# Rows of Z with 514 words instead of 528 in a two-layer graph network

## The chip, the cores and the metric

The kernel runs as one program on one core of a Trainium2 chip. The metric is device time in microseconds: the time before is the median of three executions. A fourth execution was recorded by the hardware profiler; the lines called "profile" are from it.

## The reference

There are 3125 nodes with 256 features and 50,000 directed edges (src, dst) with 16 features each; the edges are sorted by dst. Two graph layers are applied, each on the normalised, rectified nodes and each added back:

```python
# layer 0: message passing, summed at the source node
h = relu(layernorm(x))
msg = relu(concat(h[src], h[dst], edge_attr) @ mW1 + mb1) @ mW2 + mb2
agg = segment_sum(msg, src)
x = x + h + relu(concat(h, agg) @ uW1 + ub1) @ uW2 + ub2
# layer 1: three graph convolutions with self loops
h = relu(layernorm(x))
for W, b in ((W1, b1), (W2, b2), (W3, b3)):
    h = D^-1/2 (A + I)^T D^-1/2 (h @ W) + b    # gelu after the first two
x = x + h
```

## The kernel before

`mW1` has three parts, so the first product of a message is a sum of three terms: one that depends on the source node alone (table `tabA`), one on the target node alone (table `tabB`, with the bias in it) and one on the edge's features. The kernel calls **Z** the sum of the last two, 512 words for each edge. The edges come sorted by target; the sums at the source nodes need them sorted by source. So Z is written out in the order of the targets, each row to a place that belongs to its source tile, and is read back in that order.

**The array of rows.** `rows_d` (L112) lies in HBM. It has 25 tiles of source nodes (125 nodes each) of CAP = 17 x 128 rows, and spare rows behind them for edges that have no place. A row has ZW words of 4 bytes (L68): H = 512 words of Z, two words of `ends` (the source's number within its tile, plus one, and the target's number, plus one), and, before, 14 words that are zero. Nothing reads those 14.

**Stage one: blocks.** `for b in range(NB)` (L775) goes over 66 blocks of 768 edges, six columns of 128 edges each. `window` (L617) has SP load the block's two windows of `tabB` into `bw`; `features` has ACT load edge features; `prepare` (L632) makes the one-hot matrices. `block` (L656) works the six columns one after the other: GpSimd copies the block's `ends` into `zt` (L659), TensorE multiplies the one-hot matrix with the window (L666), ScalarE or VectorE copies the product into `zt` (L669), and GpSimd issues an indirect DMA that scatters the 128 rows to their places in `rows_d` (L670). `zt` is a ring of RZ = 4 buffers, each of 128 partitions x 6 rows of ZW words; the four buffers were filled with zero beyond word 514 by one GpSimd memset each (L599). They lie in memory that the tiles of the kernel's lead-in (`l1`) used, and which is given back at L591.

Rows 14 x 128 to 17 x 128 of a tile may stay without an edge. They are filled with zero by 25 DMAs of SP from the tile `zero` (L285), 384 rows each, six ahead of the blocks and the others in every second block. Scatters of the blocks from 48 on wait for all the fills.

From block 26 on (FULL_AT) the first five groups of 128 rows of every source tile are complete, and from block 29 on `first_sums` (L712) works on them beside the blocks. `rows_of` (L699) has SP load a tile's 640 rows into `xz` (L702), a ring of two buffers, one tile ahead. VectorE makes the one-hot matrices from the two words behind Z (L744 to L748), TensorE turns them and expands `tabA` (L252), VectorE adds Z (L254), ScalarE and VectorE split the rectified message in two parts (L256, L257), and TensorE sums over the edges of each source (L734). The one-hot matrices are kept for later as `oh_d`, rows of 630 half-precision words (L760). Work on the node tables (L325 to L370) is spread over the blocks ahead of block 26.

**Stage two: messages.** `messages` (L880) does the same for the other twelve groups of 128 rows of each tile, four groups in one load: `load_rows` (L891) has SP load 512 rows into `z` (L894), a ring of three buffers, two loads ahead. Beside them it counts the adjacency matrix (L950) and updates the nodes.

**Stage three.** `gcn` (L1217) is the three graph convolutions, with the adjacency matrix as the multiplied operand. It does not use the rows of Z.

The order of instructions on an engine is that of the program; the tile framework adds the waits on semaphores. DMAs of one issuing engine share a queue: q0 in the profile is GpSimd's, q1 SP's, q10 ScalarE's.

Of the kernel before, what the change touches and what calls it, by code (L numbers as in the profile page):

```python
# [45 lines left out]
N, D, H, ED, E = 3125, 256, 512, 16, 50000  # L46
# [18 lines left out]
MID = 1024  # L65
NG, AW = 7, 448
NPAD = NG * AW
ZW = 528  # L68
ROWS = NT * CAP
EPS = 1e-5  # L70
assert NT * NP == N and EP * EC == E and N <= NPAD
# [31 lines left out]
def gnn(ctx: ExitStack, tc: tile.TileContext, x, src, dst, ea, mW1, mb1, mW2, mb2, uW1, ub1, uW2,  # L103
        ub2, W1, b1, W2, b2, W3, b3, out):
    nc = tc.nc
# [5 lines left out]

    rows_d = dram.tile([ROWS + P * MB * NB, ZW], F32, name="rows_d")  # L112
    tabA = dram.tile([NR * P, H], F32, name="tabA")
# [28 lines left out]
    HALF = 13  # L142
    XZ = max(HALF * D, KP * ZW)
    xh = [g1.tile([P, XZ], F32, name="xz", bufs=2)[:, :HALF * D].rearrange("p (c f) -> p c f", f=D)
# [119 lines left out]
    with s1:  # L264
# [14 lines left out]

        zero = g1.tile([P, ZW], F32, name="zero")  # L280
        nc.gpsimd.memset(zero, 0.0)
        fills = []

        def fill(t, after=None):
            f = nc.sync.dma_start(  # L285
                rows_d[t * CAP + SURE:(t + 1) * CAP, :].rearrange("(i p) w -> p i w", p=P),
                zero.unsqueeze(1).to_broadcast([P, KT - SURE // P, ZW]))
            if after is not None:
# [274 lines left out]
        i = 2 * NT  # L563
# [32 lines left out]
        zt = []  # L596
        for i in range(RZ):
            zt.append(z1.tile([P, MB, ZW], F32, name=f"zt{i}"))
            nc.gpsimd.memset(zt[i][:, :, H + 2:], 0.0)  # L599
        EB = 6  # L600
        st, one, pay, made, evicted = {}, {}, {}, {}, {}

# [96 lines left out]
        def rows_of(t):  # L699
            v = g1.tile([P, XZ], F32, name="xz", bufs=2)[:, :KP * ZW]  # L700
            v = v.rearrange("p (k w) -> p k w", w=ZW)
            o = nc.sync.dma_start(  # L702
                v, rows_d[t * CAP:t * CAP + KP * P, :].rearrange("(k p) w -> p k w", p=P))
            tc.declare_no_dep(o.ins, group="late rows", reason="the other blocks have none of these")
            tc.add_to_no_dep_group("first loads", o.ins)
            for c in ready:
                tc.add_manual_dep(o.ins, c.ins.name, SYNC, reason="all rows are in place")
            a = a_rows[t % 2]
            nc.sync.dma_start(a, tabA[t * NP:(t + 1) * NP, :])
            return v, a  # L710
# [697 lines left out]
```

## Time and profile before

| | |
|---|---|
| median of 3 runs | 2078.67 us (2077.79 to 2092.57) |
| profiled execution | 2082.0 us |
| its span, first to last instruction | 2080.3 us |
| mean granted TensorE clock | 0.933 |
| busy, share of the span | PE 89%, PEld 67%, DVE 61%, ACT 52%, POOL 21% |
| DMA | 359.09 MB in 189,439 packets |
| q0 (GpSimd: the scatters, nearly all) | 108.12 MB, 13.5% of 16 engines' span |
| q1 (SP) | 211.58 MB, 32.0% |
| first scatter, last scatter | 71.0 us, 787.5 us |
| first load of stage two | 798.2 us |

The profile gives microseconds from the first instruction of one execution. Engines are PE (TensorE's matmuls), PEld (its weight loads, which run beside them), DVE (VectorE), ACT (ScalarE), POOL (GpSimd) and SP (which only issues DMAs). The granted clock is the share of TensorE's full clock that the throttle gave. The DMA share is the mean busy share of the core's 16 DMA engines. A line such as "L669 ACT COPY" names the line of the kernel below. A wait is written as engine, what it was about to do, "<-", and what released it; "issue" stands where the profile shows nothing that it waited for. Behind the lines the trace also has a record of every DMA packet, with its queue, its size, its start and its duration.

### The profile page before, as it was taken

To read this page: it belongs to the slowest core of one execution; us is meant where nothing else is said; L and a number is where in the kernel's file an instruction comes from. 1 tells how busy PE (TensorE), PEld (TensorE's weight loads), DVE (VectorE), ACT (ScalarE), POOL (GpSimd) and SP (SyncE) were. 2 spreads that over 40 slices of the span, in tenths; PEclk is the share of its full clock that TensorE was granted. 3 is DMA by queue.
4 is the path that set the end of the run, shared out by engine and by line. 5 is a ranking of instruction groups with operands and counts; after the bars stand their busy time and mean duration, and the time that the engine had idled before them with its cause. 6 is when DMAs were issued, how large, how long until landed. Compare 5 with 4: busy or idle time off the path is not lost. (4 is left out here: it accounts for less than half of the span.)

```text
span 2080.3 us, 28281 instructions
## 1 busy us (share of the span) xinstructions
PE 1856.0 (89%) x9183; PEld 1399.1 (67%) x9183; DVE 1271.6 (61%) x2855; ACT 1071.6 (52%) x2214; POOL 442.3 (21%) x522
## 2 busy tenths in 40 slices
PE   4788686568989996999999999999979999999997
PEld 2433343344545554688888888888867998999996
DVE  7886244455655555998888898889833223323332
ACT  3454355555666563556555565555536344434342
POOL 5466477554555441000000000000000000000000
PEclk9788898788998887999999999999989999999998
DMA  8689799897888876544544545544321000000111
GB/s 263 236 329 372 275 355 351 297 328 255 298 304 289 277 257 223 163 152 154 160 147 141 164 145 160 150 156 142 108 75 49 1 1 1 1 1 8 32 39 49
DMA packets 189439, 359.09 MB, mean 173 GB/s; under 512 B 38224, under 2 KB 67776, under 8 KB 188890
## 3 DMA queue, kind: packets, MB, share of 16 engines
q1 hardware_dynamic: 122790, 211.58, 32.0%
q0 software_dynamic: 31760, 108.12, 13.5%
q10 hardware_dynamic: 34724, 37.42, 5.3%
q8 instruction: 76, 1.25, 0.2%
q14 instruction: 89, 0.73, 0.1%
HBM read 187.51 MB, written 169.47 MB: 172 GB/s over the span
## 5 line engine op out<-in xcount | busy, mean ns | idle before, releaser
L1254 PE MATMUL p_o<-a,g 125*128 125x448 f32 x2100 | 462.8, 375 | 2.2 <-ACT g L1239 2.0
L670 POOL DMA_INDIRECT rows_d<-zt,place x391 | 388.9, 995 | 310.2 <-issue 196.6
L1254 PEld LDWEIGHTS p_o<-a,g 125*128 125x128 f32 x2100 | 391.4, 188 | 44.4 <-DVE g L1240 6.0
L256 ACT ACTIVATE m<-gb 128x512 fp32r<-128x512 f32 x425 | 265.6, 632 | 157.4 <-DVE gb L254 105.6
L257 DVE SCALAR_TENSOR_TENSOR m<-gb,m 128x512 fp32r<-128x512 f32 x425 | 287.2, 687 | 34.1 <-ACT m L256 32.4
L1249 ACT CAST a<-A 125x448 fp32r<-125x448 uint8 x263 | 148.6, 565 | 231.4 <-PE p_o L1254 231.3
L1249 DVE CAST a<-A 125x448 fp32r<-125x448 uint8 x262 | 102.8, 393 | 235.2 <-PE p_o L1254 234.3
L993 PE MATMUL p_sum<-m,oh 128*125 128x512 f32 x600 | 234.9, 434 | 6.2 <-ACT m L256 4.6
L950 PE MATMUL p_A<-od,oh_h 128*126 128x448 f16 (+3 forms) x1000 | 237.1, 327 | 1.1 <-ACT of_src L981 1.1
L252 PE MATMUL p_x<-apc,ohT 125*128 125x512 f32 x600 | 235.6, 466 | 1.3 <-ACT ohT L926 0.7
L669 ACT COPY zt<-p_z 128x512 f32<-128x512 f32 x339 | 186.9, 587 | 80.3 <-PE p_z L666 74.8
L254 DVE TENSOR_TENSOR gb<-z,p_x 128x512 f32<-128x512 f32 x300 | 202.0, 682 | 33.6 <-PE p_x L252 32.2
L666 PE MATMUL p_z<-bw,ohd 128*128 128x512 f32 x391 | 183.5, 516 | 30.6 <-DVE zt L669 12.9
L1202 POOL DMA_DIRECT2D wG<-in_L_gnn_W x3 | 2.2, 744 | 759.2 <-DVE ln_nmr L239 757.7
L734 PE MATMUL p_sum<-m,hT 128*125 128x512 f32 x250 | 110.7, 489 | 56.1 <-DVE m L257 52.6
L666 PEld LDWEIGHTS p_z<-bw,ohd 128*128 128x128 f32 x391 | 78.5, 210 | 121.7 <-issue 60.8
L950 PEld LDWEIGHTS <-oh_h 128*126 128x126 f16 x1000 | 125.6, 137 | 34.7 <-issue 1.0
L993 PEld LDWEIGHTS p_sum<-m,oh 128*125 128x125 f32 x600 | 111.7, 188 | 48.4 <-ACT m L256 21.6
L936 DVE TENSOR_SCALAR od<-iota_h,dloc 128x447 f16<-128x447 f16 (+11 forms) x300 | 138.5, 487 | 0.0
L974 ACT CAST A<-p_A 126x448 uint8<-126x448 f32 x175 | 92.9, 531 | 59.8 <-PE p_A L950 58.1
L252 PEld LDWEIGHTS p_x<-apc,ohT 125*128 125x128 f32 x600 | 109.2, 193 | 13.0 <-DVE gb L254 1.9
L356 PE MATMUL p_z<-wAB,hT 128*128 128x512 f32 (+1 forms) x200 | 111.4, 695 | 7.2 <-ACT hT L339 3.7
(268 smaller groups left out, 2748.5 us busy)
## 6 DMA issues: line engine op xcount, KB each, us to landing
z<-rows_d SPq DMA_DIRECT2D x75, 1056.0 KB
xz<-rows_d SPq DMA_DIRECT2D x25, 1320.0 KB
rows_d<-zero SPq DMA_DIRECT2D x25, 792.0 KB
tabB<-t_sb ACTq DMA_DIRECT2D x26, 512.0 KB
bw<-tabB SPq DMA_DIRECT2D x51, 256.0 KB
bw<-tabB SPq DMA_DIRECT2D x80, 128.0 KB
rows_d<-zt,place POOLq DMA_INDIRECT x391, 6.3
hT<-tabA SPq DMA_DIRECT2D x25, 250.0 KB
```

Source lines behind the costliest of these rows:

```text
L252: nc.tensor.matmul(p, ohT, apc[:NP, s, :], start=s == 0, stop=s == 1)
L254: nc.vector.tensor_add(gb, zr, p)
L256: nc.scalar.activation(m[:, 0, :], gb, AF.Relu)
L257: nc.vector.scalar_tensor_tensor(m[:, 1, :], gb, 0.0, m[:, 0, :].bitcast(F32), op0=ALU.max, op1=ALU.subtract)
L666: nc.tensor.matmul(p, one[b][:, j, :], bw[(2 * b + j // MH) % RW], start=b < WIDE, stop=True)
L669: evicted[b] = by(z[:, j, :H], p)
L670: s = nc.gpsimd.indirect_dma_start(out=rows_d, in_=z[:, j, :], in_offset=None, out_offset=bass.IndirectOffsetOnAxis(ap=place[:, j, b:b + 1 ...
L936: nc.vector.tensor_scalar(targets[k][:, :WIDTH[k]], iota_h[:, :WIDTH[k]], d_of[:, t, k:k + 1] if k < KP else dloc[t][:, k:k + 1], None, op ...
L950: nc.tensor.matmul(p_A[g][:, l - g * AW:h - g * AW], oh_h[t][:, k, :], targets[k][:, l - FIRST[k]:h - FIRST[k]], start=start, stop=stop)
L993: nc.tensor.matmul(p_sum[t], oh, m[:, s, :], start=k == KP and s == 0, stop=k == KT - 1 and s == 1)
L1249: (nc.vector.tensor_copy if turn[0] % 2 else nc.scalar.copy)(a, A[:NP, s, j * AW:(j + 1) * AW])
L1254: nc.tensor.matmul(po[:, f, :AW], g[:, s, q, f * P:(f + 1) * P], a, start=s == 0 and q == 0, stop=s == NT - 1 and q == 1)
```

## The change

A row of Z has 514 words: the 512 of Z and the two of `ends`. The array `rows_d`, the buffers `zt`, `zero`, `z` and the view of `xz` follow from the constant, and the memsets of the empty words are gone.

```diff
-ZW = 528
+ZW = H + 2
...
         for i in range(RZ):
             zt.append(z1.tile([P, MB, ZW], F32, name=f"zt{i}"))
-            nc.gpsimd.memset(zt[i][:, :, H + 2:], 0.0)
```

A row was 2112 bytes and is 2056. The buffer of `xz` keeps its size, which is set by the node features that used it before (13 x 256 words).

## The prediction

> **What bounds the kernel now.** I read the share line by slices first, then the busy time by stretches, then who waits for whom, then the DMA queues, and last the DMA packets one by one. Stage one (71 to 790 us: the blocks of 768 edges, and beside them the sums over the first five groups of rows) is where rows of Z are written; stage two (790 to 1545) only reads them; the GCN layers (1545 to 2080) do not touch them. The stages, in busy time by stretches (columns: stretch, its length, busy us and instructions of PE, weight loads, DVE, ACT, POOL, granted clock, DMA share, GB/s):
>
> ```profile
> 71.00:330.00 259.00, 202.25 (x626) 96.58 (x626) 143.62 (x342) 124.20 (x248) 165.61 (x190) 0.88 0.90 330
> 330.00:790.00 460.00, 376.27 (x1286) 215.64 (x1285) 260.89 (x498) 276.16 (x542) 240.32 (x267) 0.85 0.84 292
> 790.00:1500.00 710.00, 686.85 (x4308) 571.55 (x4309) 623.96 (x1414) 407.15 (x914) 0.00 (x0) 0.98 0.50 155
> ```
>
> In stage two PE works 687 of 710 us and DMA half the time: PE is the bound, cheaper reads of Z cannot show. In stage one no engine is full (PE 78 and 82%) and DMA stands at 0.90 and 0.84, so the transfers come closest to the bound. Finer stretches show where they are it:
>
> ```profile
> 130.00:220.00 90.00, 70.68 (x221) 33.26 (x220) 56.33 (x129) 40.11 (x81) 57.49 (x67) 0.88 1.02 378
> 220.00:250.00 30.00, 20.32 (x53) 9.87 (x52) 8.41 (x15) 10.99 (x22) 12.95 (x15) 0.73 0.55 198
> 250.00:380.00 130.00, 91.12 (x319) 49.05 (x317) 50.00 (x96) 67.12 (x136) 92.17 (x107) 0.89 0.97 349
> 380.00:480.00 100.00, 66.00 (x247) 41.64 (x248) 60.11 (x115) 57.87 (x115) 45.96 (x52) 0.80 0.82 289
> ```
>
> At 130 to 220 and 250 to 380 the 16 engines are full. The waits of 330 to 790 say who feels it:
>
> ```profile
> POOL rows_d L670 <- issue: 130.3, 106, 12.3
> DVE d_of L744 <- DMA xz<-rows_d: 77.9, 19, 14.1
> ...
> POOL rows_d L670 <- ACT zt L669: 64.0, 55, 11.4
> ```
>
> DVE waits 77.9 us in 19 of 25 tiles for a load of Z rows (xz). POOL's "issue" includes a 0.30 us gap before every scatter, even back to back; only the long ones could be a full queue. POOL has a floor of its own: a scatter is 0.96 us and that gap, so six and the copy of L659 take about 7.8 us; many blocks between 250 and 330 us start 7.8 us apart. There POOL, not DMA, may set the pace.
>
> **What the change does, part by part.**
>
> **Bytes.** A row goes from 2112 to 2056 bytes, -2.65%. From the DMA queues and issues:
>
> ```profile
> q1 hardware_dynamic: 122790, 211.58, 32.0%
> q0 software_dynamic: 31760, 108.12, 13.5%
> ...
> z<-rows_d SPq DMA_DIRECT2D x75, 1056.0 KB
> xz<-rows_d SPq DMA_DIRECT2D x25, 1320.0 KB
> rows_d<-zero SPq DMA_DIRECT2D x25, 792.0 KB
> ```
>
> The packet records of the trace give one packet's time. Scatters travel as packets of 4224 bytes (two rows), median 164 ns; a row of SP's transfers is a packet of 2112 bytes, median 86. Packets of 1024 bytes take 46 and of 2048 take 84, so a packet is 8 ns + 0.0371 ns per byte (2112 bytes: 86.4; 4224: 164.8). By that line 2056 bytes take 84.3 ns, and a pair (4112) 160.6. Estimates: -2.1 ns per row read or filled, -4.2 per pair scattered. In 71 to 790 us the trace has 24,987 pairs and 23,296 single rows (xz and fills): (24,987 x 4.15 + 23,296 x 2.1) / 16 engines = 6.5 + 3.1 = **9.5 us** of DMA time. The 38,400 rows that stage two reads save 38,400 x 2.1 / 16 = 5 us, behind PE: nothing. If that cover were gone, 5 us is all there is.
>
> **How much lies on the path.** 130 to 220 and 330 to 380 us are full: their part, 1.2 + 0.9 us, counts whole. 250 to 330 (1.2 us) is full too, but POOL keeps its 7.8 us floor: I count nothing. The remaining 6.2 us lie where the share is about 0.8: half, 3.1, because DVE waits for the load in 19 of 25 tiles. Sum 5.2, rounded **-5 us**.
>
> **Removed memsets.** Four of 168 ns on POOL at 69.7 us. The first scatter waits for ACT (70.1 us) after that, so they are covered by L669: 0. Without cover, 0.5 us once.
>
> ```profile
> 69.67 0.49 POOL L599 MEMSET zt<- 128x84 f32 x4 [21.68 <-PE bc L651]
> 70.11 0.19 POOL L659 COPY zt<-ends 128x12 f32<-128x12 f32 x1
> 71.00 1.23 POOL L670 DMA_INDIRECT rows_d<-zt,place  x1 [0.69 <-ACT zt L669]
> ```
>
> The wait for the memory's former readers (21.68 us) moves to the copy behind it on the same engine, no later. Scatters, loads and fills keep their number and order; DVE, ACT and PE handle the same elements, only at another row pitch.
>
> **Alignment, the part with no row of its own.** 2112 is 33 x 64; rows of Z start at multiples of 64 bytes now, of 8 afterwards, and neighbours share a 64-byte piece. No row of Z shows that. The nearest rows: oh_d, rows of 1260 bytes, starting at multiples of 4: 3,200 packets written, median 55 ns, mean 55.7, 90th percentile 55, while the scatters run beside them; and 3,200 read back, median 55. The line gives 54.8. hT_d, rows of 12,500 bytes, is written in 468 ns (line: 472). So an odd start costs an engine 0 to 1 ns.
>
> Two rules of the Trainium skill bear on it. "DMA: Bandwidth & Descriptors", How a descriptor splits into AXI transactions, says a read starts at the 256-byte boundary below, and bytes ahead of the row cost beats of 32 bytes. By it a row of Z now costs 66 beats + 3 of lead on average = 69, afterwards about 68.5: 0.6 ns gained instead of 2.1 per row read. But by the same rule the odd reads of oh_d would need 43.75 beats instead of 40, some 60 ns by the line's slope; they took 55, at the 10th percentile and the 90th. The row decides: 2.1. The two differ by 1.5 ns x 16,000 rows of xz / 16 = 1.5 us.
>
> The rule that speaks against the change: "Collectives: The Full Stack", Rules for kernel authors, wants buffers aligned to 32 bytes, which "Prevents HW read-modify-write". It states no price. The oh_d row does not show one, but it writes 128 neighbouring rows in a burst, not scattered rows for 700 us. Bounds per written row: below, -1 ns (the fit's spread); above, 18 ns, if each end becomes a small write of its own (the 4-byte packets take 9 ns). I take 0 to 1, the row in hand, and keep 18 for the range.
>
> **Sum.** Profiled execution: 2082.0 us (span 2080.3 and 1.7 around it), 3.3 above the median of the runs, 2078.67. 2082.0 - 5 = 2077.0; against the median, **2074 us**, -0.25%. About 1% (21 us) is what a measurement of this kernel tells from no change, so this counts as within it.
>
> **Rivals.**
>
> - **The writes pay for their ends (slower).** Place: the scatters of L670 and the fills of L285. At 18 ns per row: 24,987 pairs x 36 / 16 = +56 us, 19 fills of 384 rows x 18 / 16 = +8 us. Of the 64, the part in the full stretches (9,546 of the pairs, 38%) and half of the rest lie on the path, about +44; less the 5 gained: **2118 us**, +39. It passes 1% from 21 + 5 = 26 us on the path, that is 26 / 44 x 18 = 11 ns per row. For it: DMA is full where most scatters lie, so there is no slack, and the rule above. Against: the 55 ns of oh_d. Chance 0.38.
> - **The bytes are hidden anyway.** POOL's 7.8 us floor in the early blocks, the chain of sums later: **2079 us**. For it: POOL back to back at 250 to 330; the end of the stage (770 to 810 us) has a DMA share of 0.48. Against: the 77.9 us that DVE waits. Chance 0.12.
> - **More than the bytes comes back.** Single rows take 102.6 ns on average at a median of 86; if the queueing shrinks with the load, all 9.5 us and half of (102.6 - 86) x 23,296 / 16 = 24 us: **2057 us**. For it: full engines. Against: 2.65% less load does not halve a queue. Chance 0.04.
> - **The rows are cut.** 514 has few divisors; were each row sent as two descriptors, a scatter on POOL would take up to 0.96 us more: 391 x 0.96 = +375 us where POOL is the floor, **2450 us**. For it: nothing in the profile; rows of 630 halfwords go as one packet. Chance 0.02. That the change would not take effect at all is shut out: the row length is one constant for all three transfers.
>
> **How the numbers follow.** The forecast (0.44) and the hidden one (0.12) lie within 1%: 0.56. Slower: 0.38 + 0.02 = 0.40. Faster: 0.04. Likeliest 2074, its own range 2066 to 2083. The range must reach into the slower rival, whose price I know only from 0 to 18 ns and whose share on the path could be whole (64 - 5 = +59 us): from 2062 to 2140 about 0.17 is left out.
>
> **What would show it.** Right: packets of 2056 and 4112 bytes with medians of 84 and 160 to 161 ns, some 25,024 pairs of the latter (102.9 MB where they were 105.7), DVE's wait for xz slightly under 77.9 us, blocks still 7.8 us apart at best, stage two unchanged at 687 us of PE. Wrong: a pair of rows at 180 ns or more, a DMA share near 1 beyond 380 us, longer waits of POOL with cause "issue", the end of stage one later than 798 us. If pairs are at 160 and the stage is still longer, the price sits where packet times do not show it (landing of the scatters, now 6.3 us).

## The result, and the profile after

The change makes the kernel slower: 2102.61 us median of 6 runs (2089.92 to 2105.53), against 2078.14 for the kernel before (also 6 runs). The ratio is 1.0117, 95% interval 1.0085 to 1.0149. The profiled execution took 2105.53 us (span 2103.8, granted clock 0.925); before it was 2082.0 (span 2080.3, clock 0.933).

Of the 23.5 us between the two spans, the start of tile 0 of stage two (the first load of `oh_h`: 808.9 us before, 814.7 after) accounts for 5.8, the way from there to the same load of the last tile for 21.8 (675.1 us before, 696.9 after), and the rest of the program gives 4.1 back. So most of the loss is in stage two, where the forecast had nothing at all. From L599 on, lines of the kernel after have a number that is lower by one. The loads of `oh_h` (behind the shape: how many, the shortest, median and longest issue in ns, and the start of the first and the last), and the busy time from the first to the last of them, before and then after (columns as in the prediction):

```profile
L915 SPq DMA_DIRECT2D oh_h<-oh_d x25: 386/456/1787, 808.9 to 1484.0; - x25
808.90:1484.00 675.10, 667.21 (x4187) 555.36 (x4187) 602.67 (x1363) 393.34 (x885) 0.00 (x0) 0.99 0.50 156
...
L914 SPq DMA_DIRECT2D oh_h<-oh_d x25: 348/456/1787, 814.7 to 1511.6; - x25
814.70:1511.60 696.90, 669.62 (x4188) 556.14 (x4186) 603.67 (x1364) 394.75 (x885) 0.00 (x0) 0.99 0.48 148
```

PE does the same work in both (667 and 670 us busy), but it stands idle for 27.3 us where it stood idle for 7.9: 19.4 of the 21.8 us.

Busy time by the stretches of the prediction, of the kernel after:

```profile
71.00:330.00 259.00, 209.46 (x627) 98.52 (x628) 144.27 (x343) 125.33 (x250) 162.70 (x185) 0.86 0.89 320
330.00:790.00 460.00, 379.94 (x1270) 218.86 (x1269) 257.51 (x490) 272.42 (x535) 245.65 (x270) 0.83 0.84 287
790.00:1500.00 710.00, 666.86 (x4149) 551.73 (x4148) 604.96 (x1364) 396.06 (x884) 1.56 (x3) 0.98 0.48 150
```

In the third line PE is busy 667 of the same 710 us where it was 687, at the same clock of 0.98, with 159 fewer matmuls recorded: less of the work fits into the stretch. DMA's share is 0.48 there (0.50 before). In stage one DMA's shares are what they were or a little lower.

The queues, the DMA issues, and the waits of stage one (330 to 790 us), of the kernel after:

```profile
q1 hardware_dynamic: 122790, 207.99, 31.5%
q0 software_dynamic: 31760, 105.31, 13.1%
...
z<-rows_d SPq DMA_DIRECT2D x75, 1028.0 KB
xz<-rows_d SPq DMA_DIRECT2D x25, 1285.0 KB
```

```profile
POOL rows_d L669 <- issue: 118.9, 101, 11.8
POOL rows_d L669 <- ACT zt L668: 70.5, 61, 12.1
DVE d_of L743 <- DMA xz<-rows_d: 65.9, 17, 11.8
```

The bytes went as forecast, with the same number of packets. Packet by packet, a scattered pair (4112 bytes) has a median of 160 ns (164 before) and a single row (2056 bytes) 85 (86 before); there are 25,024 pairs. DVE's wait for `xz` fell from 77.9 us to 65.9, and POOL's waits with the cause "issue" from 130.3 to 118.9.

What is new stands in the waits of stage two (790 to 1500 us). Before:

```profile
DVE oh L917 <- DMA z<-rows_d: 13.9, 15, 1.4
...
PEld p_sum L993 <- DVE m L257: 5.2, 19, 0.5
...
PE p_sum L993 <- DVE m L257: 0.2, 1, 0.2
```

And after:

```profile
DVE oh L916 <- DMA z<-rows_d: 37.1, 24, 3.5
...
PEld p_sum L992 <- DVE m L257: 26.7, 25, 3.4
...
PE p_sum L992 <- DVE m L257: 19.5, 10, 3.0
```

DVE waits 37.1 us for loads of Z, up to 3.5 us at once, where it waited 13.9. TensorE, which bounds this stage, now waits 19.5 us for the message `m` where it waited 0.2: nearly the 21.8 us that the stage grew. The loads are not slower, though: from SP's issue to the end of the last of its 512 packets a load takes 6.25 us on average before and 6.21 after. But DVE gets to the instruction that needs the load sooner, on average 9.3 us behind the issue where it was 9.8. The order in time on DVE shows it. Before (columns: start, length, engine, line, operation, in brackets the idle time and its releaser):

```profile
1166.31 0.69 DVE L257 SCALAR_TENSOR_TENSOR m<-gb,m 128x512 fp32r<-128x512 f32 x1 [0.51 <-ACT m L256]
1166.92 0.68 DVE L254 TENSOR_TENSOR gb<-z,p_x 128x512 f32<-128x512 f32 x1
1168.30 0.68 DVE L917 TENSOR_TENSOR oh<-z,iota 128x500 fp32r<-128x500 f32 x1 [0.70 <-DMA z<-rows_d]
```

The same three instructions of another tile, after, and behind them TensorE in the same stretch:

```profile
1153.91 0.68 DVE L916 TENSOR_TENSOR oh<-z,iota 128x500 fp32r<-128x500 f32 x1 [3.52 <-DMA z<-rows_d]
1154.51 0.68 DVE L257 SCALAR_TENSOR_TENSOR m<-gb,m 128x512 fp32r<-128x512 f32 x1
1155.11 0.68 DVE L254 TENSOR_TENSOR gb<-z,p_x 128x512 f32<-128x512 f32 x1
```

```profile
1155.25 0.79 PE L992 MATMUL p_sum<-m,oh 128*125 128x512 f32 x1 [2.96 <-DVE m L257]
```

Before, DVE works `m`, `gb`, `oh`; after, `oh`, `m`, `gb`. The one-hot matrix `oh` needs a load of Z that has not landed; `m` and `gb` need nothing of that load, but they stand behind `oh` on the same engine and start only after it, and TensorE's sum waits for `m`. The instructions of the two compiled programs, compared engine by engine, confirm that this is the rule and not an accident of one tile: in stage two, DVE has the order m, gb, oh in 24 places and oh, m, gb in one before, and in 13 and 19 after. GpSimd's order is the same in both programs; TensorE's, ScalarE's, DVE's and SP's differ. Nothing in the diff asks for that. The order is not written in the kernel's text: the tile framework chooses it when it builds the program, and for the kernel after it chose another. Whether the shorter rows or the missing memsets moved it was not separated, since no run has one without the other. The sentence of the kernel's description above, that the order of instructions on an engine is that of the program, is wrong.

### The profile page after: what moved, and what is told of

Read it like the earlier page. It is cut to its first block, busy times and chain, and to the rows that moved or that the text cites. A ratio compares the mean times of both kernels' runs of the same rounds, so it can differ in the third digit from the quotient of the medians.

```text
span 2103.8 us, 28241 instructions
## 1 busy us (share of the span) xinstructions
PE 1868.4 (89%) x9183; PEld 1407.6 (67%) x9183; DVE 1270.6 (60%) x2855; ACT 1073.3 (51%) x2214; POOL 447.0 (21%) x518
## 3 DMA queue, kind: packets, MB, share of 16 engines
q1 hardware_dynamic: 122790, 207.99, 31.5%
q0 software_dynamic: 31760, 105.31, 13.1%
## 4 chain that ended last, share of the span: by engine, by line
PE 64%; DMA 20%; DVE 11%; issue 2%; ACT 1%; POOL 1%; SPq 0%; another core or an unknown queue 0%; ACTq 0%; DVEq 0%; POOLq 0%
PE p_o L1253 20%; DMA xz<-rows_d 8%; PE p_x L252 7%; PE p_A L949 6%; DMA z<-rows_d 6%; PE p_sum L992 5%; PE p_z L356 3%; PE p_z L665 3%; PE p_g L1236 3%; PE p_z L664 2%; PE p_sum L733 2%; PE nd L841 2%; PE nd L854 2%; PE nd L863 2%; DVE gb L254 2%
## 5 line engine op out<-in xcount | busy, mean ns | idle before, releaser
L992 PE MATMUL p_sum<-m,oh 128*125 128x512 f32 x600 | 235.5, 436 | 22.5 <-DVE m L257 19.5
```

Of the source, the lines that this page charges most:

```text
L992: nc.tensor.matmul(p_sum[t], oh, m[:, s, :], start=k == KP and s == 0, stop=k == KT - 1 and s == 1)
```

## The experiments

The theories. **O**, the order: the loss comes from the order that the framework gives the changed program, above all from `oh` (also called the mask) ahead of `m` on DVE; the row length by itself costs nothing. **W**, the writes: rows of 2056 bytes pay for ends that do not fill 32-byte pieces (the slower rival of the prediction), in whatever order.

To separate them, a kernel builds both programs, reads off the order of every engine in one, and imposes it on the other by dependencies that exist only while the program is built: they fix who comes first on an engine and add no wait on the chip. Each is compared with the kernel before on the same chip, in five rounds. Three chips were used, and they differ in speed by more than the change does (the kernel before has medians from 2078 to 2111 us), so ratios are compared and not times.

### Short rows, the order of before

```diff
-    nc = bacc.Bacc(...)                        # one program
+    ORDER[:] = order_of(program(528)[0])       # each engine's order with rows of 528 words
+    nc, arrays = program(514)                  # rows of 514 words
...
+    for k, places in ORDER:
+        if k > 0:       # both parts of the program
+            for a, b in zip(places, places[1:]):
+                tc.add_manual_dep(here[MADE[b]], MADE[a], FREE, reason="the other program's order")
```

> Rows of 514 words, with every engine's instructions in exactly the order that the kernel before has. Theory O (the planner that orders the instructions prices a shorter transfer lower, and so laid out another order; that order costs the time, the rows save a little): ratio to before 0.995 to 1.000, 2068 to 2079 us, the first load of stage two at 792 to 798 us, stage two's loads 28.3 us a tile. Theory W (the writes pay for ends that share a 64-byte piece): the time stays with the rows, 1.009 to 1.015, 2097 to 2109 us.

Measured: ratio 0.9992, interval 0.9971 to 1.0013 (2107.03 us against 2108.03 on that chip). From tile 0 to the last, stage two takes 677.9 us. The loss is gone with the rows still short. W's price, if there is one, is no larger than what the bytes bring, to within the interval.

### Long rows, the order of after

The same with the two widths exchanged: rows of 528 words with their memsets, in the order of the kernel after.

> The mirror image: rows of 528 words, with every engine's instructions in the order that the changed kernel has. Theory O: the time stays with the order, ratio 1.010 to 1.016, 2099 to 2111 us, and DVE waits some 35 us in stage two for loads of Z rows. Theory W: 0.998 to 1.003, 2074 to 2084 us.

Measured: 1.0083, interval 1.0052 to 1.0114, a little under the 1.010 to 1.016 expected. Not a byte of the change is in this kernel, and it has the change's waits:

```profile
DVE oh L917 <- DMA z<-rows_d: 36.2, 19, 3.2
...
PEld p_sum L993 <- DVE m L257: 26.3, 22, 3.0
...
PE p_sum L993 <- DVE m L257: 19.8, 10, 2.6
```

The order is enough to make some seven tenths of the loss. That is O, and it shuts out W as its main cause.

### Which part of the order: stage one or the rest

Two kernels take stage one in one order and everything behind it in the other.

```diff
     for k, places in ORDER:
-        if k > 0:       # both parts of the program
+        if k > 1:       # stage two and what follows; stage one stays as the framework orders it
```

First, 514 words with the order of before from stage two on:

> Rows of 514 words; stage one in the changed kernel's order, stage two and the convolutions in the order of the kernel before. If O holds and the loss is made in stage two by its order (there the two profiles part by 21 us, in stage one by 6): stage one ends some 6 us later than before and stage two costs no more than before, ratio 1.000 to 1.004, 2078 to 2087 us. If stage two is slow because of what stage one hands over, or because of the rows: 1.009 to 1.015, 2097 to 2109 us.

Measured: 0.9993, interval 0.9973 to 1.0014. Second, 528 words with the order of after from stage two on:

> Rows of 528 words; stage one in the order of the kernel before, stage two and the convolutions in the changed kernel's order. If the order of stage two carries the loss: ratio 1.007 to 1.012, 2093 to 2103 us, with the first load of stage two at 798 us as before. If it does not (W, or an effect of stage one): 0.998 to 1.002, 2074 to 2082 us.

Measured: 1.0082, interval 1.0058 to 1.0106. The order of stage one shows no effect, within intervals of 0.2% each way; the effect of the order comes from stage two on. An effect of stage one of up to some 6 us (0.3%) would not show here, so the 5.8 us by which stage two starts later in the profile of after have no shown cause. They are within what single profiles differ by: the kernel with the mask put back and the changed kernel run again (both below) have the same orders in stage one and ran on one chip, and their first loads of `oh_h` start at 804.6 and 812.2 us.

### The mask put back

The kernel after, in its own order on every engine, except that on DVE in stage two each `oh, m, gb` becomes `m, gb, oh`:

```diff
-        oh (L916)   m (L257)   gb (L254)
+        m (L257)    gb (L254)  oh (L916)
```

> The changed kernel in its own order, but on VectorE, in stage two, the 19 places where a one-hot (oh) stands right ahead of a message's split (m) and the next message's sum (gb) are turned round to m, gb, oh, as the kernel before mostly has it. Theory H (VectorE waits in order for a load of Z rows at oh, and m and gb stand behind it; TensorE waits for m): ratio to before 0.998 to 1.004, VectorE waits no more than 20 us for loads of Z rows in stage two, stage two 28.3 to 28.6 us a tile. If the order of TensorE or ScalarE carries the loss: 1.007 to 1.014.

Measured: 1.0043, interval 1.0023 to 1.0062; the change itself, run again on that chip (below), 1.0114. Moving this one instruction, in 19 places, gives back 0.7 of the 1.1%; 1.0043 is just above the 0.998 to 1.004 expected if the place of `oh` on DVE were all. The waits of this kernel in stage two say what is left:

```profile
DVE oh L917 <- DMA z<-rows_d: 14.5, 20, 1.4
...
PEld tr L924 <- DVE oh L917: 12.6, 8, 1.6
...
PE tr L924 <- DVE oh L917: 9.4, 9, 1.1
...
PEld p_sum L993 <- DVE m L257: 3.6, 14, 0.5
```

The waits for the load and for `m` are those of before. In their place TensorE waits for `oh`: its own order still has the transposes of `oh` (L924), for 12 of the 75 loads, earlier among its sums than in the kernel before. That fits the remaining 0.4%, but no run changed TensorE's order alone, so it is not shown.

### The mask moved ahead in a kernel that is not slow

The opposite: short rows in the order of before, with each of the 24 `m, gb, oh` turned into `oh, m, gb` on DVE, and nothing else moved.

> Rows of 514 words in the order of the kernel before, with the reverse move: in stage two the 24 places where VectorE has m, gb, oh become oh, m, gb. Theory H: the loss comes back with this move alone, ratio 1.006 to 1.014, VectorE waits 30 us or more for loads of Z rows in stage two. If the place of oh does not matter: 0.996 to 1.002, as with this order unmoved (0.9992).

Measured: 1.0296, interval 1.0263 to 1.0330, the expected direction and twice the expected size; stage two takes 729.5 us from tile 0 to the last. In its waits:

```profile
PEld p_sum L993 <- DVE m L257: 51.8, 33, 3.3
...
DVE oh L917 <- DMA z<-rows_d: 46.6, 22, 3.2
PE p_sum L993 <- DVE m L257: 44.3, 21, 3.1
```

Against the same kernel without the move (0.9992 and 0.9981 on other chips), 3% from one instruction of 0.68 us placed ahead of two others in 24 places. PE's own wait of 44.3 us is most of the 54 us by which the stage is longer than in the kernel before. The rest is that PE is busy for 678.9 us where it was 667.2, at a granted clock of 0.98 where it was 0.99; why was not tested.

### Other row lengths in the order of before

With the order held, the row length can be varied alone. Rows of 544 words (2176 bytes, a multiple of 32):

```diff
-    nc, arrays = program(514)
+    nc, arrays = program(544)
```

> Rows of 544 words (2176 bytes, a multiple of 64 as 2112 is), in the order of the kernel before: 3.0% more bytes a row. If bytes of Z rows lie on the path as the prediction had it (half of the DMA time, -5 us for 56 bytes): +6 us, ratio 1.003. If they are hidden: 0.999 to 1.001. If the full DMA time counts: 11 us, 1.005.

Measured: 1.0073, interval 1.0045 to 1.0102, more than the 1.003 expected. That left open whether short rows gain less than bytes are worth, because of their ends, so three lengths were run together on another chip: 520 words (a multiple of 32 bytes), 546 (not one), and 514 again.

> Rows of 520 words (2080 bytes, a whole number of 32-byte pieces) with every engine held to the order of the kernel before. The step from 528 to 544 words in that order cost 0.73%, 0.046% a word; 514 words in it gave 0.08%. If the price is one of bytes and rows of 2056 bytes pay for ends that are not whole pieces, 520 words show what the bytes alone are worth: 8 x 0.046%, ratio 0.996 (2070 us). If bytes under 2112 are hidden and no ends are paid for, 0.999 to 1.000. In both the tiles of stage two stay at 28.3 us; the difference shows in the time of stage two's first load.

> Rows of 546 words (2184 bytes, not a whole number of 32-byte pieces), order of the kernel before. By bytes alone 18 x 0.046% = 0.8%, ratio 1.008, beside 1.0073 of 544 words (2176 bytes, whole pieces). If the ends of a row are paid for as much as 514 words would have to pay to lose their 0.6%, 1.014. Against 1.008 it would be the alignment that matters, near 1.008 it is not.

> Rows of 514 words in the order of the kernel before, once more, on the chip of the two beside it: 0.9992 as the first time if bytes under 2112 bring nothing; 0.994 if the 0.046% a word that 544 words cost holds below 528 too and the first time was low by chance.

Measured: 520 words 0.9970 (0.9946 to 0.9994), 546 words 1.0042 (1.0020 to 1.0064), 514 words 0.9981 (0.9962 to 1.0000). Alignment does not order them: 546 words cost no more than 544 (on another chip), and 514 and 520 cannot be told apart. The price of 0.046% a word, taken from the 544 words, did not hold: 546 words cost half of the 1.008 that it asked for, and the 0.994 that it asked for with 514 words lies outside the interval.

The load that starts tile 0 of stage two tells how long everything ahead of it took. On the chip of the 544-word kernel it starts at 804.7 us with 514 words (the kernel with the mask ahead) and at 815.5 with 544: 10.7 us for 30 words. On the chip of the other three it starts at 837.1 us with 514 words, 840.5 with 520 and 851.9 with 546: 14.8 us for 32 words. The prediction's 5.2 us for 14 words make 11.1 and 11.9. These are single profiles, and two of the same rows and the same order in stage one differed by 7.6 us (804.6 and 812.2 above), so the agreement in size is no proof. The packets agree: pairs have medians of 160 to 161 ns with 514 words, 161 with 520, 168 with 544 and 169 with 546, where the prediction's line gives 160.6, 162.3, 169.5 and 170.1.

### The change once more

The kernel after, unchanged, on the chip on which the mask was put back and moved ahead and rows of 544 words ran.

> The changed kernel itself, beside the other three on one chip. Its ratio was 1.0117 (1.0085 to 1.0149); with the rows of 514 words at the old order worth 0.9992 and the new order with rows of 528 words at 1.0083, both theories say 1.007 to 1.012 here; above 1.012 the rows and the order would add to more than their sum.

Measured: 1.0114, interval 1.0074 to 1.0154, with DVE waiting 37.5 us for Z and TensorE 18.9 us for `m`. The loss repeats with its waits.

The best version found is 520 words in the order of before, 0.9970, whose interval (to 0.9994) only just leaves out 1. Rows of 514 words in that order are at 0.9992 and 0.9981, both intervals reaching to 1.

## Why the prediction was right or wrong

**The step that failed** is the sentence at the end of the memsets' paragraph: "Scatters, loads and fills keep their number and order; DVE, ACT and PE handle the same elements, only at another row pitch." Number and elements held. The order did not: TensorE's, DVE's, ScalarE's and SP's instructions came in another one, and that costs 0.83% with the old rows, some 17 us: the forecast put a term at nothing that is larger than all its others. In stage two PE's wait for `m` went from 0.2 to 19.5 us. From the same belief came "cheaper reads of Z cannot show" in stage two. That the loads are not the bound there is right (DMA's share is 0.48); but the place in DVE's order at which it needs a load decides whether TensorE feels it, and the prediction never put that place in question. Its checks did contain the right alarm, "stage two unchanged at 687 us of PE": it reads 667. The measured 2102.61 us lies inside the stated range of 2062 to 2140, but that is luck: the range was stretched upward for the ends of written rows, which showed no such price.

**The bytes (−5 us)**: right in mechanism, and in size as far as the runs resolve it. Packets cost 160 and 85 ns where 160 to 161 and 84 were forecast. At equal order the two runs of 514 words give 0.9992 ± 0.0021 and 0.9981 ± 0.0019; their mean is 0.9987 ± 0.0014 (half-widths combined as independent), or −3 ± 3 us of 2080. The forecast of −5 us lies in that, and 0 lies at its edge. Rows of 520 words gain 0.30% (0.06 to 0.54). The longer rows show the price better: 544 and 546 words lose 0.73% and 0.42%, where 5.2 us for 14 words would make 0.29 and 0.32.

**The memsets (0)**: their cover was as told. The wait for the memory's readers moved to the copy behind them:

```profile
70.54 0.19 POOL L658 COPY zt<-ends 128x12 f32<-128x12 f32 x1 [21.91 <-PE bc L650]
72.17 1.23 POOL L669 DMA_INDIRECT rows_d<-zt,place  x1 [1.44 <-ACT zt L668]
```

The first scatter still waits for ScalarE; it starts 1.2 us later than before, but POOL's own copy, with no memset ahead of it, is done 1.44 us before that start.

**Alignment (0 to 1 ns taken, 18 kept for the range)**: right, as far as packet times go, to take the measured row of `oh_d`. A scattered pair of 2184-byte rows has a median of 169 ns, one of 2176 bytes 168. The rule of the Trainium skill ("Collectives: The Full Stack", Rules for kernel authors), that buffers aligned to 32 bytes avoid a read-modify-write, may hold for what it speaks of; no run here shows a price for rows of Z.

**The rivals.** "The writes pay for their ends" forecast the right sign for the wrong reason: by its own sign, pairs at 180 ns or more, it did not happen. Its other signs do not carry it either: stage two did start later (first load at 804.2 us, 798.2 before), by no more than single profiles differ, and the median time from the issue of a scatter to its landing is 6.5 us (6.3 before; 6.4 with 514 words in the old order and 6.4 with 544). A price of the ends of a few microseconds, about what the bytes bring, is not excluded. "The bytes are hidden anyway" is not excluded by the 514-word runs; the 520-word rows, which gain, and the longer rows, which cost time, speak against it. "More than the bytes comes back" is out: single rows still average 104.6 ns at a median of 85 (102.6 at 86). "The rows are cut" is out: the packets number 122,790 and 31,760 as before. What happened was not among them.

**What stays open.** The change costs 1.17 and 1.14% in its two comparisons; the order alone cost 0.83 and 0.82% on another chip and the bytes bring 0.1, so the change costs 0.4% more than their sum. The intervals (1.0074 to 1.0154 against 1.0052 to 1.0114) overlap, and the change itself was not run on the chip of the order runs, so this may be chips or chance. Why 544 words cost more than 546 is in the same case. The move of `oh` costs 3.0% in 24 places but gives back only 0.7% in 19; TensorE waits for `m` 21 times in the kernel with the mask ahead and 10 times in the changed one, and no run shows why. Whether another buffer for `z` would take the waits out of either order was not tried.

## What to carry to other kernels

Where a framework orders the instructions, a change of a transfer's size or of the list of instructions can also be a change of order; compare the two compiled orders engine by engine before you credit or blame the bytes, and hold the order fixed to measure the bytes. On an engine that starts its instructions in the program's order, as the traces here show DVE doing, look for the instruction that waits for a load and ask who stands behind it: an operation of 0.68 us, moved ahead of two that the bounding engine needs, in 24 places, cost 3% here. A stage in which DMA is busy half the time can still lose to a transfer, where the instruction that waits for it has something urgent behind it.

## What the runs showed of the hardware that was not expected

The price of up to 18 ns a row that had been kept open does not show in packet times: pairs of rows of 2056, 2080, 2176 and 2184 bytes fall on the prediction's line within 2 ns, whether or not the rows are multiples of 32 bytes. What bytes are worth seems to depend on how fast the engines go: on the chip of the 520- and 546-word kernels their profiles have a granted clock of 0.81 and 0.78 and a DMA share of 0.80 at 71 to 330 us, and 18 words more cost 0.42%; on the chip of the 544-word kernel, with 0.88 and 0.91, 16 words more cost 0.73%. Those intervals overlap too, so this is a hint and no more.
